# A decoder layer on one core: DMA transposes replaced by TensorE transposes and by VectorE transposes of 32-row squares with plain DMAs, in a new instruction order

## The chip, the cores and the metric

The kernel runs on one core of a Trainium2 chip. The metric is the device time of one execution in microseconds; the median over several runs is compared. Five engines run side by side, each with its own queue in program order: TensorE (PE in the profile; its weight loads are listed as PEld), VectorE (DVE), ScalarE (ACT), GpSimd (POOL) and SyncE (SP), which here only issues DMAs. Semaphores tie the queues together.

## The reference

The reference is one decoder layer over x of 16 sequences x 128 tokens x 256 features:

```
x = x + attn(layernorm(x))            # 16 heads of 64; fixed point: every product truncated to 1/4096
x = x + xattn(layernorm(x), ctx)      # 16 heads of 64, keys and values from ctx (16, 128, 128)
x = x + ffn(layernorm(x))             # 256 -> 1024 -> 256, two rank-16 experts, relu, weighted sum
```

In the first attention q, k, v, the scores, the softmax and the output go through `make_fxp`, a clip to about +-8 and a truncation to multiples of 1/4096, so those values are integers up to a scale. The second attention is ordinary softmax attention on a context. Everything is float32 outside.

## The kernel before

The 16 sequences are handled in 8 blocks (`blk`) of two sequences, 256 tokens. Each block passes through the first attention ("A"), the second ("B") and the feed-forward part ("C"). The attentions are done in two halves (`hf`) of eight heads, and within a half for one sequence (`b`) at a time. So there are 8 x 2 x 2 = 32 tiles of attention probabilities in A and 32 in B, each 128 queries x (8 heads x 128 keys).

Float32 operands are split into a high and a low f16 part (names ending in `h` and `l`), and a product takes three f16 passes. Where values are exact integers a float32 product is used.

The steps that the change and the prediction touch, with their lines in the kernel before:

- **Layer norm and input transpose**, `prep` (from L419). The normalized tile `xh` has tokens on the partitions; the following products need features there. For three of the 24 calls (`BY_PE`: A of blocks 0 and 1, C of block 7) TensorE transposes four 128x128 float32 squares into PSUM (`pt`, L449), and ScalarE and VectorE read the two f16 parts out of PSUM (L451, L452). For the other 21, ScalarE and VectorE make the two parts first (`xhi` L455, `xlo` L456) and two transposing DMAs move them (L457, L458).
- **Products q, k, v of A**, `attn_A` (from L543). Weights are scaled by 256. ScalarE reads each PSUM result twice (`trunc`, L507 and L508: the positive and the negative part, truncated into int16), and VectorE subtracts (L525 for q and k; L553 for v, to float32).
- **Probabilities of A.** After the exponential (L562) and the row sum (L564), GpSimd multiplies each head with its reciprocal and truncates to int16 (`a_A`, L571). One transposing DMA moves the tile (L574), GpSimd casts it to float32 (`aTf_A`, L576), and TensorE multiplies with v (`av_A`, L583).
- **Scores and probabilities of B**, `attn_B`. TensorE makes the scores (L540), VectorE the row extremes (`mx_B`, L641), ScalarE the exponentials and their sums (L645). GpSimd normalizes (L660) and rounds to f16 (`ah_B`, L661), VectorE subtracts for the low part (`al_B`, L662). Two transposing DMAs (L669) bring `aTh_B` and `aTl_B` for the product `av_B` (L679).
- **Output and feed-forward**: `out_proj` (`pj_A`, `pj_B`, L607), `ffn` (`u_C` L761, `dn_C` L799, the output `xo` L806 and its DMA).

The code does not run in the order in which it is written. Each step is recorded as an operation on an engine, `place` checks the dependencies along a written list of some 2,000 operation numbers (`ORDER`) and hands out buffers along it, and `emit` issues the operations in that order. The costs in the calls (`a_op`, `v_op`, `g_op`, `p_op`, `d_op`) do not enter the program. There are four sizes of SBUF buffers, `SLOTS = {"L": (4096, 9), "M": (2048, 25), "S": (1024, 26), "T": (64, 16)}` (bytes per partition and number), and two of PSUM, `PSLOTS = {"big": (4096, 3), "sml": (2048, 2)}`. A tile takes the next free buffer of its size at its first operation in the order, so an operation also waits for the last reader of the tile that had the buffer before.

Of the kernel before, what the change touches and what calls it, by code (L numbers as in the profile page):

```python
# [8 lines left out]
F32 = mybir.dt.float32  # L9
F16 = mybir.dt.float16  # L10
# [24 lines left out]
BY_PE = (("A", 0), ("A", 1), ("C", 7))  # L35
NORM_B = "PP"
# [3 lines left out]
1 29 84 85 2 20 323 86 87 324 3 14 5 0 22 325 4 326 17 88 11 327 89 6 8 15 31 90 18 91 12 7 30 42 328 92 94 93 9 19  # L40
98 99 39 16 13 23 802 100 101 10 95 149 150 142 143 102 103 40 152 151 96 104 97 54 33 126 145 144 26 562 447 128
110 153 329 127 105 111 112 106 146 41 563 147 154 129 32 148 108 113 337 330 45 155 130 338 107 131 114 564 132 109
133 43 448 44 134 331 115 381 1042 116 565 382 803 340 339 117 566 449 118 384 388 567 383 385 386 389 56 333 341
332 390 334 177 387 391 392 342 135 156 208 568 178 569 335 119 161 393 1043 804 179 157 120 621 163 162 180 394 336
164 622 628 181 182 159 158 46 623 121 624 136 183 416 160 184 165 55 185 57 137 47 1282 417 629 625 166 626 418 395
396 186 24 122 627 25 343 635 138 209 631 636 167 419 123 398 397 630 51 187 638 168 400 188 577 169 59 637 139 632
805 420 344 633 345 402 401 189 140 578 584 421 27 210 585 170 1044 347 580 579 403 171 124 634 58 190 365 346 349
586 587 172 570 366 191 173 367 28 571 192 35 36 399 581 219 351 174 422 350 404 368 175 220 141 125 640 176 423 424
34 352 405 406 369 639 370 641 193 353 407 425 642 194 643 48 354 573 221 355 454 196 371 222 455 356 195 197 198
656 37 408 456 1283 426 427 199 409 657 658 253 806 200 38 201 410 457 202 52 203 807 659 572 687 205 53 254 204 372  # L50
206 215 216 255 660 574 411 373 257 256 258 217 661 428 374 218 662 249 348 259 250 644 211 429 212 645 1045 688 251
357 252 663 808 49 60 375 261 646 260 809 927 213 376 1046 262 412 647 377 358 868 413 214 582 430 664 378 263 869
359 274 275 861 50 862 575 871 870 264 223 872 360 648 414 265 379 224 276 266 588 863 817 864 277 361 865 362 225
818 363 380 875 415 364 873 819 665 583 431 876 1048 236 278 576 666 878 237 279 877 267 226 866 432 649 820 867 238
268 874 589 879 605 227 433 896 21 591 590 667 606 821 810 239 434 607 668 1522 898 811 228 269 270 592 229 1762 897
650 669 435 593 230 651 812 813 1047 822 492 880 232 231 608 271 436 1763 240 899 824 882 609 652 881 493 241 594
825 242 1284 1049 437 438 272 653 243 207 494 439 1064 440 61 595 670 826 1065 814 596 233 827 1057 495 458 459 441
1058 597 244 273 900 245 610 1066 815 1067 883 1050 598 442 611 1051 1523 816 460 823 280 443 1068 246 234 612 1060
1059 461 884 235 901 1052 1053 671 829 445 845 599 247 600 885 613 847 444 846 654 828 488 282 831 489 902 830 490
601 496 497 281 450 614 886 498 451 1054 615 248 283 1285 903 491 500 602 1055 63 1286 1061 499 616 452 501 284 655  # L60
1108 904 453 1109 1101 617 618 1287 285 1102 502 513 1110 1111 1524 1056 603 619 832 620 887 64 604 446 905 503 888
833 462 906 848 1104 889 672 286 62 673 504 1112 1525 1103 514 1113 1289 1526 1115 1062 65 463 834 515 1063 849 1116
1288 835 505 464 1105 506 674 507 287 1118 1106 1069 836 1117 516 1107 1527 1167 1071 465 675 850 851 475 837 890
509 1529 476 288 1297 517 1070 477 1085 838 928 508 1114 1086 891 478 289 676 1087 290 466 1072 892 907 518 1120 66
908 1298 1119 893 1348 519 1121 839 1349 1300 909 467 1088 1122 840 1299 1528 510 521 1089 1351 1350 1136 852 68 468
929 469 1123 1341 677 1342 479 520 678 1290 1291 1647 511 1137 81 1138 480 471 841 1355 1764 1356 470 1352 1090 1073
894 842 481 1293 853 843 512 1091 1292 522 1344 1343 1139 472 1092 482 523 82 1301 1544 1357 1302 1358 69 1545 483
484 524 473 1546 854 83 679 70 1530 1303 1124 1547 1294 1295 680 1531 1093 1296 525 1304 1074 474 1533 1305 1353
1309 1532 855 1075 71 1345 1325 689 856 1306 844 1307 485 1327 1094 1326 486 1346 1537 1140 1311 910 72 857 1076
1538 1347 1125 487 78 1141 1354 972 1142 1328 291 1077 911 973 526 1534 292 1143 1535 1310 974 1078 895 1407 527 976  # L70
1540 858 1308 1539 1144 977 293 1329 859 975 860 1588 79 1589 1079 528 1145 1126 73 978 1095 1330 681 1360 979 1127
1541 1312 1096 1331 1536 1591 682 74 294 1590 1097 912 1542 1313 67 694 1543 686 1361 695 683 1098 75 1128 1362 1765
696 295 1080 1332 1565 1314 80 1549 685 697 684 913 76 1566 698 1081 1359 699 1146 1550 1567 690 1551 915 1315 1129
1363 691 77 1568 1581 1592 700 1593 1364 1316 692 701 914 1582 693 1130 1376 1317 1082 1318 1569 702 1147 1570 1365
1584 703 1583 1377 1148 1131 1149 1333 529 1319 1378 1132 530 1133 728 704 1595 1379 1366 1596 1585 916 1134 705
1150 531 1594 1598 1552 729 1597 1135 1151 1099 1766 1571 532 730 1083 1320 715 1100 732 1380 1084 733 1548 1367
1767 731 1553 1368 1152 1334 1768 533 736 716 1586 706 1321 1572 535 734 1587 737 738 735 1573 739 1769 917 1381
1153 1554 1322 1555 1600 717 1616 297 534 1770 1335 1154 1556 1771 296 1382 1601 1602 740 1618 1155 1617 1336 938
918 939 1773 1772 1574 298 741 1369 940 1156 1383 1603 1157 707 1337 718 1557 1777 1778 919 941 934 1558 299 1370
1338 719 536 742 1780 935 1575 1599 1779 1371 936 753 300 1158 1339 920 1576 754 301 921 1577 922 302 720 937 743  # L80
923 1559 1372 1373 1168 924 309 1384 310 708 1619 925 1578 303 755 721 1374 304 1560 1561 1774 1385 537 722 968 1775
305 1386 969 1340 1562 311 312 540 756 306 724 1387 538 1323 1324 1620 723 710 970 1781 744 709 971 541 1388 1389
711 539 930 1604 1782 1390 1776 1783 931 313 542 314 543 712 725 932 544 757 1391 1789 726 745 1805 933 1605 545
1791 1784 1806 1606 1807 1790 1375 1607 727 758 1785 980 993 759 1621 1787 1786 994 1159 1808 713 746 1392 981 1160
995 548 996 747 1393 714 307 982 1608 549 942 1161 550 1162 955 315 1622 1609 1394 308 997 1623 316 1395 318 1164
1169 956 551 1610 1163 546 317 547 1396 1165 1397 1624 943 957 319 552 1887 748 958 944 760 1212 1208 749 1213 553
1209 1214 1611 983 321 762 554 750 1579 1216 1210 751 1217 1612 959 1625 1215 1809 960 1211 1792 752 1821 1822 1626
1828 761 1218 1823 1810 984 945 1580 1613 555 1793 1829 998 1398 763 1219 1824 961 764 1825 765 1627 1628 1830 946
1408 1629 1220 1399 1400 1826 1233 1221 985 1234 1831 986 766 1630 1827 1832 1174 767 962 1401 963 947 1833 1175
1614 1222 768 1170 1648 1171 1563 988 556 1235 1834 987 964 1788 1176 1172 948 1177 1173 1402 769 1840 1856 1223 965  # L90
1409 1835 1842 1841 1811 1836 1403 1236 966 1404 989 1857 1166 949 1858 1837 1414 1838 1224 1405 926 1415 1631 558
1182 770 1794 1225 1615 1843 771 1859 1237 951 990 1410 1564 1812 967 1411 950 991 999 1416 1860 992 557 1226 1412
952 1183 1417 1413 1238 1000 1184 560 1195 1406 1185 1196 1239 1844 953 1227 1422 1001 1197 1423 1178 1179 1632 1198
1424 1845 1240 1199 1633 1813 1186 1180 1002 1846 1418 1187 1229 1795 1861 954 1634 1200 772 1181 1649 1419 1242
1435 1003 1635 1796 1241 1448 1228 1436 1243 1004 1005 1420 322 1814 1230 1636 1637 1201 1244 1425 1797 1421 1815
1231 1232 1449 1437 1456 1457 1202 1006 1188 1203 1245 1847 1798 1816 1007 1452 1458 1204 1190 1848 1799 1438 1453
1862 1638 1459 1450 1189 1451 1191 1008 1658 1639 1817 1454 1863 1659 1818 1640 1800 1192 1692 1839 1849 1660 1801
# [19 lines left out]
1037 2003 1521 1992 1986 1760 1761 2008 2010 1040 2004 1041 2012 2007 2005 2006 2009 2011 2013 2014 2015 2017 2016  # L117
2018
"""
WPOOL = ()  # L120
SPLIT_C = (7,)
WARM = 16

# [22 lines left out]
class Recorder:  # L146
    def __init__(self):
        self.ops = []
# [738 lines left out]
```

## Time and profile before

| | |
|---|---|
| median of 3 runs | 542.34 us (540.81 to 542.90) |
| the profiled execution's own time | 543.11 us |
| its span on the core | 541.3 us |
| granted TensorE clock | 1.00 |
| DMA transposes | 138 (32 `aT_A`, 64 `aTh_B` and `aTl_B`, 42 of layer-norm outputs) |

The span is the time from the first to the last instruction of the program. In the page, an engine's busy time does not count waits, branches and the issue of DMAs. In a line of a group of instructions the entries are: line of the code, engine, operation, output <- inputs (shapes), count | busy time in us, mean duration of one in ns | idle time of the engine just before them, and what ended it. In the busy time by stretches, the engines follow in the order PE, PEld, DVE, ACT, POOL, each with its number of instructions, then the granted clock, the DMA engines' share and GB/s. In a list of waits the three numbers are the total in us, the times, and the longest. In the timeline the first number is the start in us and the second the length.

### The profile page before, as it was taken

How to read it: one execution, taken by the hardware profiler on the slowest of the kernel's cores; microseconds unless marked ns; L12 is line 12 of the kernel's file. 1: busy time of each engine (PE TensorE's matmuls, PEld its weight loads, DVE VectorE, ACT ScalarE, POOL GpSimd, SP SyncE). 2: the span in 40 equal slices, each digit the busy share in tenths (PEclk: the TensorE clock that was granted, in tenths of full speed). 3: DMA queues.
4: the chain of work that ended last, by engine and by line, in shares of the span. 5: the costliest groups of instructions: out<-in, count | busy, mean ns of one | idle time of the engine just before them, and what ended most of it. 6: DMA issues, size and time to landing. Idle time of an engine off the chain costs nothing. (4 is left out here: it accounts for less than half of the span.)

```text
span 541.3 us, 15415 instructions
## 1 busy us (share of the span) xinstructions
PE 514.0 (95%) x6144; PEld 417.8 (77%) x6144; DVE 491.7 (91%) x818; ACT 457.9 (85%) x1014; POOL 337.5 (62%) x413
## 2 busy tenths in 40 slices
PE   7989997998989999999999999999999999999997
PEld 6777575877678876877777788877878788887886
DVE  5999899999999999999999988999989998986663
ACT  5999999999999999998998997879676998846331
POOL 1057436965667778646586797578967276847440
PEclk9999999999999999999999999999999999999999
DMA  8812504334452474423336126346935722691011
GB/s 283 295 41 58 142 16 107 70 60 81 75 73 51 98 148 78 99 69 41 62 76 99 23 43 106 61 79 103 150 59 105 127 51 53 116 155 22 11 40 59
DMA packets 137453, 47.17 MB, mean 87 GB/s; under 512 B 125988, under 2 KB 134438, under 8 KB 137382
## 3 DMA queue, kind: packets, MB, share of 16 engines
q1 hardware_dynamic: 137382, 46.20, 42.2%
q8 instruction: 48, 0.79, 0.6%
q14 instruction: 23, 0.19, 0.1%
HBM read 13.41 MB, written 2.10 MB: 29 GB/s over the span
## 5 line engine op out<-in xcount | busy, mean ns | idle before, releaser
L571 POOL TENSOR_SCALAR a_A<-E_A,rc_A 128x128 int16<-128x128 f32 x256 | 123.3, 503 | 49.6 <-DVE rc_A L566 27.5
L645 ACT ACTIVATE E_B<-s_B,mx_B 128x128 f32<-128x128 f32 x256 | 91.1, 419 | 6.7 <-DVE mx_B L641 3.8
L660 POOL TENSOR_TENSOR E_B<-E_B,rc_B 128x1024 f32<-128x1024 f32 x32 | 65.9, 2063 | 36.2 <-DVE rc_B L648 31.8
L645 ACT ACTIVATION_READ_ACCUMULATOR E_B<-s_B,mx_B 128x1 f32 x256 | 64.8, 259 | 0.0
L576 POOL TENSOR_SCALAR aTf_A<-aT_A 128x1024 f32<-128x1024 int16 x32 | 37.9, 1185 | 31.3 <-DMA aT_A<-a_A 18.1
L489 PEld LDWEIGHTS <-wh_A 128*128 128x128 f16 x512 | 49.2, 98 | 10.4 <-issue 2.7
L661 POOL TENSOR_SCALAR ah_B<-E_B 128x1024 f16<-128x1024 f32 x32 | 43.0, 1349 | 11.4 <-DVE al_B L662 5.7
L662 DVE TENSOR_TENSOR al_B<-E_B,ah_B 128x1024 f16<-128x1024 f32 x32 | 43.5, 1365 | 0.9 <-POOL ah_B L661 0.9
L641 DVE TENSOR_REDUCE mx_B<-s_B 128x8 f32<-128x1024 f32 x32 | 38.6, 1210 | 3.7 <-PE s_B L540 3.7
L564 DVE TENSOR_REDUCE sm_A<-E_A 128x8 f32<-128x1024 f32 x32 | 38.4, 1205 | 2.2 <-ACT E_A L562 2.2
L583 PE MATMUL av_A<-aTf_A,v_A 128*64 128x128 f32 x512 | 34.5, 278 | 4.2 <-POOL aTf_A L576 2.8
L508 ACT ACTIVATE n_sA<-s_A 128x1024 int16<-128x1024 f32 x32 | 36.6, 1183 | 2.1 <-PE s_A L540 2.1
L562 ACT ACTIVATE E_A<-p_sA 128x1024 f32<-128x1024 int16 x32 | 37.0, 1178 | 0.4 <-DVE r L779 0.4
L507 ACT ACTIVATE p_sA<-s_A 128x1024 int16<-128x1024 f32 x32 | 37.2, 1181 | 0.0
L761 PE MATMUL u_C<-xTl_C,wh_Ci 128*128 128x256 f16 x128 | 34.9, 273 | 1.2 <-DMA xTl_C<-xlo_C 1.2
L489 PE MATMUL gk_A<-xTh_A,wh_A 128*128 128x256 f16 x128 | 35.0, 273 | 1.0 <-ACT p_gA L507 0.8
L489 PE MATMUL gq_B<-xTh_B,wh_Bq 128*128 128x256 f16 x128 | 34.9, 273 | 0.9 <-DVE kl_B L625 0.8
L489 PE MATMUL gq_B<-xTl_B,wh_Bq 128*128 128x256 f16 x128 | 34.9, 272 | 0.7 <-DMA xTl_B<-xlo_B 0.7
L489 PE MATMUL gq_A<-xTl_A,wh_A 128*128 128x256 f16 x128 | 34.9, 272 | 0.5 <-DVE xTl_A L452 0.5
L761 PE MATMUL u_C<-xTh_C,wh_Ci 128*128 128x256 f16 x128 | 34.9, 273 | 0.3 <-DVE kl_B L625 0.3
L489 PE MATMUL gq_A<-xTh_A,wh_A 128*128 128x256 f16 x128 | 34.9, 273 | 0.2 <-DVE kl_B L625 0.2
L607 PE MATMUL pj_B<-wh_Bo,oh_B 128*128 128x256 f16 x128 | 34.9, 273 | 0.0
(213 smaller groups left out, 2004.4 us busy)
## 6 DMA issues: line engine op xcount, KB each, us to landing
st_A<-in_wqkvT_dram SPq DMA_DIRECT2D x6, 512.0 KB, 7.4
X<-in_x_dram SPq DMA_DIRECT2D x8, 256.0 KB, 6.3
out_dram<-xo SPq DMA_DIRECT2D x16, 128.0 KB, 1.7
st_Ap<-in_wprojT_dram SPq DMA_DIRECT2D x2, 512.0 KB, 9.3
cst<-in_ctxT_dram SPq DMA_DIRECT2D x8, 128.0 KB, 2.8
st_Bq<-in_Wq_dram SPq DMA_DIRECT2D x2, 512.0 KB, 4.3
st_Bo<-in_Wo_dram SPq DMA_DIRECT2D x2, 512.0 KB, 3.9
st_Ci<-in_wiT_dram SPq DMA_DIRECT2D x2, 512.0 KB, 3.8
```

Source lines behind the costliest of these rows:

```text
L489: PE.matmul(o[:, c, :], wv(w, i)[:, k + k0, c * 128:(c + 1) * 128], cols(acts[j], k), start=(n == 0), stop=(n == 3 * nk - 1))
L507: a_op(ncol, lambda: S.activation(p(), view(ps()), AF.Relu, bias=-LAM, scale=scale), [ps], [p], name="p")
L562: a_op(1024, lambda p=p, e=e: S.activation(flat(e()), p(), AF.Exp, bias=0.0, scale=1.0 / 4096.0), [p], [e], name="exp")
L564: v_op(1024, lambda e=e, sm=sm: V.tensor_reduce(sm(), e(), axis=AX.X, op=ALU.add), [e], [sm], name="sum")
L571: G.tensor_scalar(a()[:, h * N:(h + 1) * N], e()[:, h, :], r()[:, h:h + 1], -LAM, ALU.mult, ALU.add)
L576: g_op(1.02, lambda aT=aT, af=af: G.tensor_scalar(af(), aT(), 2.0 ** -12, 0.0, ALU.mult, ALU.add), [aT], [af], name="cast")
L641: v_op(1024, lambda ps=ps, mx=mx: V.tensor_reduce(mx(), ps(), axis=AX.X, op=ALU.min), [ps], [mx], name="max")
L645: S.activation(e()[:, h, :], ps()[:, h, :], AF.Exp, bias=mx()[:, h:h + 1], scale=-1.0, accum_out=sm()[:, h:h + 1])
L660: g_op(1.87, lambda e=e, r=r: G.tensor_tensor(e(), e(), r().unsqueeze(2).to_broadcast([128, HH, N]), ALU.mult), [r], [e], name="norm")
L661: g_op(1.02, lambda e=e, ah=ah: G.tensor_scalar(ah(), flat(e()), 1.0, 0.0, ALU.mult, ALU.add), [e], [ah], name="ahi")
L662: v_op(1024, lambda e=e, ah=ah, al=al: V.tensor_tensor(al(), flat(e()), ah(), ALU.subtract), [e, ah], [al], lock=True, name="alo")
L761: PE.matmul(ps()[:, c, :], wv(w, i)[:, k, c * 128:(c + 1) * 128], cols(xt[j], k), start=(n == 0), stop=(n == 6))
```

## The change

No DMA transposes remain; there are three replacements.

- `prep` has only the TensorE path: all 24 calls transpose on TensorE through a small PSUM buffer.
- In A, the probabilities are made with an offset of 1024, so that the int16 bits, read as f16, are transposed unchanged by TensorE against an f16 identity (`ident16`), eight heads into one small PSUM buffer (`tp_A`); ScalarE casts that to float32 (`CAST_A = "AA"`). GpSimd's cast is gone.
- In B, VectorE transposes each normalized tile in squares of 32x32 (`t1_B`), 16 plain DMAs of 32 partitions x 256 float32 carry the squares to their places (`t2_B`), and only then the tile is split into the f16 parts, on GpSimd and VectorE (`TR_B = "VV"`, `ALO = "V"`).

Besides, the weights of A are scaled by 4096 in place of 256, and v of A takes one pass on ScalarE, one on VectorE (`trunc1`) and a clamp on GpSimd instead of two on ScalarE and a subtraction on VectorE. `ORDER` is a new list. The numbers given as costs were changed in many calls. Other new branches (`S32_A`, `S32_B`, `HH_A`, `int_32`, `score_32`, `f32`, the "P" branch of `TR_B`) are switched off by their settings.

```diff
-BY_PE = (("A", 0), ("A", 1), ("C", 7))
-NORM_B = "PP"
 ORDER = """
 ...
+S32_A = ()
+S32_B = ()
+HH_A = ()
+TR_B = "VV"
+ALO = "V" 
+CAST_A = "AA"
 ...
+    ident16 = const.tile([128, 128], F16, name="ident16")
+    S.copy(ident16, ident)
 ...
-            load_weight(f"A{t}{hf}", kc(wqkvT[:, c0:c0 + 512]), 512)
+            load_weight(f"A{t}{hf}", kc(wqkvT[:, c0:c0 + 512]), 512, ws=4096.0)
 ...
-        if (key, blk) in BY_PE:
-            ps = tl("pt_" + key, "sml", [128, BLK, 2, N], F32)
-            ...
-        else:
-            xi, xl = tl("xhi_" + key, "S", [128, BLK * D], F16), tl("xlo_" + key, "S", [128, BLK * D], F16)
-            a_op(512, lambda: S.copy(xi(), fx()), [xh], [xi], name="xhi")
-            v_op(512, lambda: V.tensor_tensor(xl(), fx(), xi(), ALU.subtract), [xh, xi], [xl], lock=True, name="xlo")
-            d_op(230, lambda: SP.dma_start_transpose(th().rearrange("p b c n -> p (b c) n"), xi()), [xi], [th], name="T")
-            d_op(230, lambda: SP.dma_start_transpose(tlo().rearrange("p b c n -> p (b c) n"), xl()), [xl], [tlo], name="T")
+        ps = tl("pt_" + key, "sml", [128, BLK, 2, N], F32)
+
+        def tr():
+            for b in range(BLK):
+                for c in range(2):
+                    PE.transpose(ps()[:, b, c, :], xh()[:, b, c * 128:(c + 1) * 128], ident)
+        p_op(0.44, tr, [xh], [ps], name="tr")
+        a_op(512, lambda: S.copy(th(), ps()), [ps], [th], name="th")
+        v_op(512, lambda: V.tensor_tensor(tlo(), ps(), th(), ALU.subtract), [ps, th], [tlo], name="tl")
 ...
         v = tl("v_A", "L", [128, BLK, 512], F32)
-        pv, nv = tl("p_gA", "M", [128, 1024], I16), tl("n_gA", "M", [128, 1024], I16)
-        trunc(v_ps, pv, nv, 1024, 4096.0 / WS)
-        v_op(1024, lambda: V.tensor_tensor(flat(v()), pv(), nv(), ALU.subtract), [pv, nv], [v], lock=True, name="v")
+        trunc1(v_ps, 1024, "gA", lambda p: g_op(1.12, lambda: G.tensor_scalar(flat(v()), p(), -32767.0, None, ALU.max), [p], [v], name="v"))
 ...
-                    G.tensor_scalar(a()[:, h * N:(h + 1) * N], e()[:, h, :], r()[:, h:h + 1], -LAM, ALU.mult, ALU.add)
+                    G.tensor_scalar(a()[:, h * N:(h + 1) * N], e()[:, h, :], r()[:, h:h + 1], 1024.0 - LAM, ALU.mult, ALU.add)
             g_op(8 * 0.35, norm, [e, r], [a], name="norm")
-            aT = tl("aT_A", "M", [128, HH, N], I16)
-            d_op(460, lambda a=a, aT=aT: SP.dma_start_transpose(aT(), a()), [a], [aT], name="T")
+            tp = tl("tp_A", "sml", [128, HH, N], I16)
+            def tr(a=a, tp=tp):
+                for h in range(HH):
+                    PE.transpose(tp()[:, h, :].bitcast(F16), a()[:, h * N:(h + 1) * N].bitcast(F16), ident16)
+            p_op(8 * TR16, tr, [a], [tp], name="trA")
             af = tl("aTf_A", "L", [128, HH, N], F32)
-            g_op(1.02, lambda aT=aT, af=af: G.tensor_scalar(af(), aT(), 2.0 ** -12, 0.0, ALU.mult, ALU.add), [aT], [af], name="cast")
+            if CAST_A[b] == "A":
+                a_op(1024, lambda tp=tp, af=af: S.activation(flat(af()), flat(tp()), AF.Identity, bias=-0.25, scale=2.0 ** -12), [tp], [af], name="cast")
 ...
-            ah, al = tl("ah_B", "M", [128, HH * N], F16), tl("al_B", "M", [128, HH * N], F16)
 ...
-                g_op(1.02, lambda e=e, ah=ah: G.tensor_scalar(ah(), flat(e()), 1.0, 0.0, ALU.mult, ALU.add), [e], [ah], name="ahi")
-                v_op(1024, lambda e=e, ah=ah, al=al: V.tensor_tensor(al(), flat(e()), ah(), ALU.subtract), [e, ah], [al], lock=True, name="alo")
 ...
-            for s_, a in (("h", ah), ("l", al)):
-                t = tl(f"aT{s_}_B", "M", [128, HH, N], F16)
-                d_op(460, lambda t=t, a=a: SP.dma_start_transpose(t(), a()), [a], [t], name="T")
+                t1, t2 = tl("t1_B", "L", [128, 4, HH, 32], F32), tl("t2_B", "L", [128, 4, HH, 32], F32)
+                v_op(1024, lambda e=e, t1=t1: V.transpose(t1(), e().rearrange("p h (j b) -> p j h b", b=32)), [e], [t1], name="tr32")
+                for i in range(4):
+                    def mv(i=i, t1=t1, t2=t2):
+                        for j in range(4):
+                            SP.dma_start(t2()[32 * j:32 * j + 32, i], t1()[32 * i:32 * i + 32, j])
+                    R.op("SP", 2.0, mv, [t1], [t2], lat=3.8, name="mv", bw=128 / 330.0)
+                aT = [tl(f"aT{s_}_B", "M", [128, 4, HH, 32], F16) for s_ in "hl"]
+                g_op(1.12, lambda t2=t2, aT=aT: G.tensor_scalar(aT[0]().rearrange("p i h b -> p (i h b)"), t2().rearrange("p i h b -> p (i h b)"), 1.0, 0.0, ALU.mult, ALU.add), [t2], [aT[0]], name="ahi")
+                ...
+                    v_op(1024, lambda t2=t2, aT=aT: V.tensor_tensor(f(aT[1]), f(t2), f(aT[0]), ALU.subtract), [t2, aT[0]], [aT[1]], lock=True, name="alo")
```

## The prediction

> **What bounds the kernel now.** I read the page first (busy time by engine), then the busy time by stretches, the groups of instructions, VectorE's timeline and the chain of waits.
>
> ```profile
> PE 514.0 (95%) x6144; PEld 417.8 (77%) x6144; DVE 491.7 (91%) x818; ACT 457.9 (85%) x1014; POOL 337.5 (62%) x413
> ```
>
> TensorE and VectorE are both near the span of 541.3 us. TensorE's records overlap, so its 95% overstates it; VectorE's 491.7 is real occupation. The stretches show who sets the end, and when (columns: length, then busy of PE, PEld, DVE, ACT, POOL):
>
> ```profile
> 0.00:20.00 20.00, 16.93 (x124) 15.17 (x125) 13.80 (x31) 14.40 (x18) 2.28 (x10) 1.00 0.91 313
> 20.00:457.50 437.50, 418.67 (x5179) 333.44 (x5177) 418.70 (x716) 401.57 (x911) 295.01 (x381) 1.00 0.43 80
> 457.50:541.30 83.80, 78.43 (x847) 69.20 (x844) 59.15 (x73) 41.91 (x89) 40.22 (x22) 1.00 0.34 69
> ```
>
> Up to 457.5 us VectorE works 13.80 + 418.70 = 432.5 us and idles 25.0. After that VectorE thins out (59 of 84), and TensorE works 78.4 of 83.8, idling 5.4. So I read the span as a cut: VectorE's work up to the cut, then TensorE's work behind it: 432.5 + 25.0 + 78.4 + 5.4 = 541.3. What is added to VectorE ahead of the cut, or to TensorE behind it, is paid in full unless the idle 30.4 shrinks.
>
> **What the change takes and gives, VectorE first.** For each of the 32 tiles of the second attention a 32-row transpose of 128x1024 f32 is added. No row shows one. The nearest rows read one f32 tile of 1024 columns or write one:
>
> ```profile
> L641 DVE TENSOR_REDUCE mx_B<-s_B 128x8 f32<-128x1024 f32 x32 | 38.6, 1210 | 3.7 <-PE s_B L540 3.7
> L662 DVE TENSOR_TENSOR al_B<-E_B,ah_B 128x1024 f16<-128x1024 f32 x32 | 43.5, 1365 | 0.9 <-POOL ah_B L661 0.9
> L553 DVE TENSOR_TENSOR v_A<-p_gA,n_gA 128x1024 f32<-128x1024 int16 x16 | 21.8, 1362 | 0.5 <-ACT p_gA L507 0.5
> ```
>
> Neighbouring records overlap, so what one costs in a full queue is the step from start to start:
>
> ```profile
> 450.57 1.23 DVE L641 TENSOR_REDUCE mx_B<-s_B 128x8 f32<-128x1024 f32 x1 [0.70 <-PE s_B L540]
> 451.71 1.21 DVE L625 SCALAR_TENSOR_TENSOR ql_B<-gq_B,qh_B 128x1024 f16<-128x1024 f32 x1
> 452.84 1.22 DVE L641 TENSOR_REDUCE mx_B<-s_B 128x8 f32<-128x1024 f32 x1
> ```
>
> That is 1.14 and 1.13. I take 1.14: 32 x 1.14 = +36.5. Low end: the copies of 1024 int16 (L526 qh_A, 471 ns), 32 x 0.47 = 15.0. High end: the slowest 1024-column row (L779, 1610 ns), 51.5. A gain is excluded, since the instruction replaces none on VectorE: the subtraction that forms the low half (L662) stays, one per tile, the same size.
>
> The first attention's v (L553, 1362 ns) becomes one instruction that reads PSUM, like L625 vl_B (1204): 16 x -0.16 = -2.5. Of the input transposes 21 go over from DMA to TensorE, so xlo (6.5 + 6.1 + 4.1 = 16.7 us in all) becomes a read of PSUM like L452 (686 ns): 21 x 0.69 = 14.5, so -2.2. Sum: 491.7 + 36.5 - 2.5 - 2.2 = 523.5. In the changed order two of the 32 transposes stand behind its cut, so 30 x 1.14 - 2.5 - 2.0 = +29.7 count ahead of it.
>
> **TensorE.** Removed: nothing. Added: 256 f16 transposes (eight for each of 32 tiles, with a weight load each) and 21 x 4 f32 ones. Four f32 ones take 0.44 us in the chain of waits, so 21 x 0.44 = 9.2:
>
> ```profile
> 509.62 0.44 PE pt_C L449 x4
> ```
>
> For f16 the nearest is the score product: on 64-row halves it starts eight every 0.225 us, records of 217 ns overlapping:
>
> ```profile
> 269.65 0.39 PE L540 MATMUL s_A<-kl_A,qh_A 64*128 64x128 f16 x8
> 269.87 0.39 PE L540 MATMUL s_A<-kh_A,qh_A 64*128 64x128 f16 x8
> ```
>
> Two halves run side by side, so a full 128x128 is 0.056 us: 256 x 0.056 = 14.4, high end the f32 price of 0.11, 28.2; low end half, 7.2, if they also overlapped. TensorE gains 23.6, to 537.6 busy by its records. It stays the second engine ahead of the cut; behind it two more groups of pt_C stand than now: +0.9.
>
> A wait moves, too. TensorE's transposes of a_A wait for GpSimd. Until now it was SP's transposing DMA that waited there, with only other DMAs queued behind it:
>
> ```profile
> SPq L574 <- POOL a_A L571: 43.6, 11, 10.2
> ```
>
> On TensorE whatever product comes next in its queue would be held up instead, and VectorE behind that. I cost it at nothing because the new order can put the transposes after other products, as it does now with the products av_A, which wait 4.2 us in all for the same chain (L583); bare, the bound is those 43.6 us.
>
> The Trainium skill, "TensorE: Matmul & The Clock Gate", Part 4, gives about 275 ns for a 128x128 bf16 transpose inside a kernel. By that the 256 would cost 70.4 us and TensorE alone would need over 590; the trace's 217 ns records that start 28 ns apart say that such a figure is a latency, so I do not use it.
>
> **The others.** ScalarE: 32 casts from PSUM like L507 p_sA (1181 ns) +37.8, the second pass over v gone -18.7, the 21 casts xhi (L455, 13.3 us in all) now at xTh's 562 ns (L451) -1.5: 475.5, under VectorE and so covered. GpSimd: 32 casts gone (L576) -37.9, 16 clamps of v at that row's 1185 ns +19.0: 318.6; it is covered by VectorE, and if it were not it would gain. SP: 138 transpose issues of about 1.2 us (some 168 us) go, 512 small moves come. A plain DMA's issue is 0.316 us for 16 rows and 0.380 for an output:
>
> ```profile
> L372 SPq DMA_DIRECT2D lora_sb<-in_loraBT_dram x8: 315/316/347, 21.9 to 50.3; - x8
> DMA to landing us min/median/max: 2.0/2.5/4.2
> ```
>
> 512 x 0.32 to 0.38 = 162 to 195 us on SP, no more than now in kind. But one tile needs 16 in a row: 5.1 to 6.1, and 2.5 to land, some 8 us instead of the 3.2 that a transposed tile now takes to land. The moves wait for VectorE's transpose; queued behind them on SP are the next tile's moves, the context loads and the outputs, all due later. Then GpSimd, VectorE and TensorE wait in that order. The work of other tiles hides the extra 5 us; were it bare once, at the last tile, it would cost 5.
>
> The Trainium skill, "DMA: Bandwidth & Descriptors", Rules for kernel authors, speaks against such moves: under 64 KB a transfer is mostly overhead, and these are 32 KB. No row of this size is in the trace; by the rule the price lies in the issue and landing times above and not in bytes, so it would alter the sum by the bare 5 us at most.
>
> **Relief.** VectorE's durations lie above their group medians by 42.8 us in all (al_B: mean 1365, median 1210). GpSimd's stretch too (a_A up to 1850 ns, median 376), so part may be mutual hindrance. GpSimd loses 18.9 of 337.5 busy, VectorE 37 instructions of two SBUF inputs. Bounds 0 and -42.8; I take a tenth, -4, near the share of work that goes.
>
> **The sum.** 29.7 + 0.9 - 4 = +26.6 on the profiled span: 541.3 + 26.6 = 567.9. The profiled execution took 543.11 and the median of the runs is 542.34, 0.8 below it; 542.34 + 26.6 = **569**. It assumes that the new order idles as the old one does, 30.4 us around the cut. Even with 12 less it is 557.
>
> **Rivals.**
> - *Hindrance goes.* No crossbar writes, 32 fewer casts on GpSimd: VectorE's 42.8 us of stretch vanish. Then 541.3 + 30.6 - 42.8 = 529. It decides from a relief of over 31 of the 42.8. Against: 94% of GpSimd's busy time remains. Faster: 0.06. Halfway, with relief near 31, no change (within 0.5%, about what a measurement of this kernel can tell): 0.04.
> - *TensorE becomes the bound.* f16 transposes at 0.11: +28.2 + 9.2 = 37.4, and the new PSUM tiles (32 tp_A, 21 pt) queue for the two small PSUM buffers or wait for a_A. 514.0 + 37.4 plus its present idle 27.3 = 579. For: both engines are nearly full, and SP's 43.6 us of waiting for a_A; against: scores already run at half that price. 0.20.
> - *Buffers.* t1 and t2 take two more of the nine 4 KB buffers per tile, held through the 8 us of moves; new idle of 8 to 17: 576 to 586. The profile shows no wait for a buffer now. 0.15.
> - That transposing DMAs remain is excluded: the changed order has none.
>
> **Numbers.** My forecast has 0.55 and its own range 551 to 575: transposes at 0.5 us would give 569 - 19 = 550, at 1.61 583, so the outer range 550 to 587 holds those, TensorE's case and the buffers'. Slower 0.90, same 0.04, faster 0.06.
>
> **What would show it.** After: VectorE busy about 520 to 524; a transpose row of 32 near 1.2 us; tp_A rows on TensorE starting about 56 ns apart; ScalarE near 475, GpSimd near 319; no DMA transposes, DMA share far down. Wrong if VectorE falls under 500, if its rows other than the transpose shrink by tens of us, or if TensorE, not VectorE, has the least idle time ahead of the last 70 us.

## The result, and the profile after

The changed kernel takes 645.42 us (median of 4 runs, 643.98 to 646.37) where the kernel before took 542.62 in the same session (540.81 to 543.39): 102.8 us more, a ratio of 1.190 (95% interval 1.186 to 1.194). The forecast was 569 with a range of 550 to 587. The sign was right and the size was not. The profiled execution took 643.98 us, with a span of 642.1 and a granted clock of 0.963 where it was 1.00 before.

The busy times by engine come out almost as forecast:

```profile
PE 561.3 (87%) x6484; PEld 453.4 (71%) x6484; DVE 517.7 (81%) x850; ACT 477.9 (74%) x1031; POOL 312.8 (49%) x397
```

VectorE was forecast at 523.5, ScalarE at 475.5, GpSimd at 318.6. TensorE's 561.3 hold the lower clock: 642.1 x (1 - 0.963) = 23.8 us, if TensorE was busy in all of it, and without them it is at 537.5 (forecast 537.6). So no engine works much longer than forecast. The span of each engine is filled up with idle time: VectorE idles 124.4 us of it instead of 49.6.

The busy time by stretches, cut at the same places as before:

```profile
0.00:20.00 20.00, 16.86 (x118) 13.43 (x119) 12.30 (x26) 14.39 (x18) 3.87 (x11) 1.00 0.91 315
20.00:457.50 437.50, 387.56 (x4602) 308.20 (x4601) 378.00 (x650) 364.34 (x748) 235.51 (x328) 0.96 0.15 42
457.50:642.10 184.60, 156.84 (x1771) 131.75 (x1769) 127.43 (x176) 99.14 (x267) 73.44 (x58) 0.96 0.17 47
```

Up to 457.5 us every engine does less than before in the same time (VectorE 378.0 in place of 418.7, TensorE 387.6 in place of 418.7), though over the whole span all but GpSimd have more to do. Something holds all of them. The chain that ended last names it (shares of the span by engine, then by line):

```profile
SPq 29%; PE 28%; DVE 15%; ACT 8%; issue 7%; POOL 7%; DMA 5%; POOLq 0%; DVEq 0%; ACTq 0%
SPq L708 28%; PE pj_B L638 4%; DMA t_B<-t_B 4%; PE gk_A L493 4%; PE dn_C L849 3%; DVE aTl_B L716 3%; POOL a_A L594 3%; PE gq_B L493 2%; PE gq_A L493 2%; DVE t_B L704 2%; PE u_C L808 2%; DMA st_A<-in_wqkvT_dram 1%; ACT E_A L585 1%; PE s_A L564 1%; DVE mx_B L679 1%
```

Before, SP's queue had a share of 0%, though that chain could be followed back only to 485 us. Line L708 is the loop that issues the 16 moves of a tile. Asked for by itself, the line shows the duration of one issue (ns, min/median/max), and its landing:

```profile
L708 SPq DMA_DIRECT2D t_B<-t_B x512: 507/589/1835, 100.9 to 590.2; - x171
DMA to landing us min/median/max: 1.7/1.8/3.8
```

And SP's own timeline, late in the program (start, length, count):

```profile
504.80 40.48 SPq L708 DMA_DIRECT2D t_B<-t_B  x61
```

61 moves back to back in 40.48 us, 0.66 us each. Between 360 and 600 us the same line shows how long SP waited before its moves (the second row, ns):

```profile
L708 SPq DMA_DIRECT2D t_B<-t_B x337: 507/589/1762, 359.6 to 590.2; - x169
L708 SPq EVENT_SEMAPHORE  x26: 17/17/28, 360.2 to 572.6; - x26
```

No wait is longer than 28 ns: from 360 us on, each tile's transpose is already done when SP comes to its moves. 337 moves in 231 us are one tile per 11 us. The list of waits shows who stands behind it (total us, times, longest), and the groups show GpSimd's idle time ahead of the split:

```profile
POOL aTh_B L711 <- DMA t_B<-t_B: 97.7, 19, 10.1
...
ACT oh_B L732 <- PE av_B L726: 37.5, 14, 8.2
...
DVE aTl_B L716 <- POOL aTh_B L711: 23.8, 8, 5.3
...
DVE aTl_B L716 <- DMA t_B<-t_B: 16.6, 6, 6.7
...
DVE t_B L704 <- DMA t_B<-t_B: 10.9, 4, 7.2
```

The last of these is VectorE's transpose. Its input comes from no DMA, so this is read as waiting for a buffer that earlier moves have not yet emptied.

### The profile page after: what moved, and what is told of

The parts are those of the page before. It is cut to its first block, busy times and chain, and to the rows that moved or that the text cites. A ratio compares the mean times of both kernels' runs of the same rounds, so it can differ in the third digit from the quotient of the medians.

```text
span 642.1 us, 16573 instructions
## 1 busy us (share of the span) xinstructions
PE 561.3 (87%) x6484; PEld 453.4 (71%) x6484; DVE 517.7 (81%) x850; ACT 477.9 (74%) x1031; POOL 312.8 (49%) x397
## 4 chain that ended last, share of the span: by engine, by line
SPq 29%; PE 28%; DVE 15%; ACT 8%; issue 7%; POOL 7%; DMA 5%; POOLq 0%; DVEq 0%; ACTq 0%
SPq L708 28%; PE pj_B L638 4%; DMA t_B<-t_B 4%; PE gk_A L493 4%; PE dn_C L849 3%; DVE aTl_B L716 3%; POOL a_A L594 3%; PE gq_B L493 2%; PE gq_A L493 2%; DVE t_B L704 2%; PE u_C L808 2%; DMA st_A<-in_wqkvT_dram 1%; ACT E_A L585 1%; PE s_A L564 1%; DVE mx_B L679 1%
## 5 line engine op out<-in xcount | busy, mean ns | idle before, releaser
L594 POOL TENSOR_SCALAR a_A<-E_A,rc_A 128x128 int16<-128x128 f32 x256 | 106.0, 434 | 52.2 <-DVE rc_A L589 16.6
L711 POOL TENSOR_SCALAR aTh_B<-t_B 128x1024 f16<-128x1024 f32 x32 | 34.4, 1076 | 112.5 <-DMA t_B<-t_B 97.7
L687 POOL TENSOR_TENSOR E_B<-E_B,rc_B 128x1024 f32<-128x1024 f32 x32 | 62.2, 1946 | 44.8 <-DVE rc_B L686 38.0
L716 DVE TENSOR_TENSOR aTl_B<-t_B,aTh_B 128x1024 f16<-128x1024 f32 x32 | 47.3, 1482 | 40.4 <-POOL aTh_B L711 23.8
L576 POOL TENSOR_SCALAR v_A<-p_gA 128x1024 f32<-128x1024 int16 x16 | 48.0, 3003 | 31.3 <-DVE p_gA L518 16.6
L493 PEld LDWEIGHTS <-wh_A 128*128 128x128 f16 x512 | 50.3, 101 | 16.3 <-issue 6.2
L704 DVE STREAM_TRANSPOSE t_B<-E_B 128x1024 f32<-128x1024 f32 x32 | 39.5, 1234 | 14.1 <-DMA t_B<-t_B 10.9
L726 PEld LDWEIGHTS <-vh_B 128*64 128x64 f16 x512 | 24.8, 121 | 35.5 <-issue 25.4
L732 ACT ACTIVATE oh_B<-av_B 128x512 f16<-128x512 f32 x32 | 19.4, 612 | 37.8 <-PE av_B L726 37.5
L726 PE MATMUL av_B<-aTh_B,vh_B 128*64 128x128 f16 x256 | 27.5, 240 | 20.9 <-POOL aTh_B L711 12.2
L605 ACT ACTIVATE aTf_A<-tp_A 128x1024 f32<-128x1024 int16 x32 | 33.4, 1054 | 4.9 <-DMA t_B<-t_B 2.4
```

Source lines behind the costliest of these rows:

```text
L493: PE.matmul(o[:, c, :], wv(w, i)[:, k + k0, c * 128:(c + 1) * 128], cols(acts[j], k), start=(n == 0), stop=(n == 3 * nk - 1))
L576: trunc1(v_ps, 1024, "gA", lambda p: g_op(1.12, lambda: G.tensor_scalar(flat(v()), p(), -32767.0, None, ALU.max), [p], [v], name="v"))
L594: G.tensor_scalar(a()[:, h * N:(h + 1) * N], e()[:, h, :], r()[:, h:h + 1], 1024.0 - LAM, ALU.mult, ALU.add)
L687: g_op(1.87, lambda e=e, r=r: G.tensor_tensor(e(), e(), r().unsqueeze(2).to_broadcast([128, HH, N]), ALU.mult), [r], [e], name="norm")
L704: v_op(1024, lambda e=e, t1=t1: V.transpose(t1(), e().rearrange("p h (j b) -> p j h b", b=32)), [e], [t1], name="tr32")
L716: v_op(1024, lambda t2=t2, aT=aT: V.tensor_tensor(f(aT[1]), f(t2), f(aT[0]), ALU.subtract), [t2, aT[0]], [aT[1]], lock=True, name="alo")
```

## Experiments on the moves

Theory 1: SP issues the 512 moves one after the other at 0.59 us each, some 10 us a tile, and paces the second attention. Rivals: TensorE's added transposes in two small PSUM buffers (2), VectorE's transposes of squares (3), the clamps of v on GpSimd and the new order (4). Each kernel here is the changed kernel but for the edit shown.

**Four moves a tile, the same bytes.**

```
-                        for j in range(4):
-                            SP.dma_start(t2()[32 * j:32 * j + 32, i], t1()[32 * i:32 * i + 32, j])
+                        SP.dma_start(t2()[:, i], t1()[:, i])
```

> The same bytes leave in four moves of 128 rows per tile in place of sixteen of 32 rows (128 issues on SP in place of 512). Left out: the squares stay on their own rows, so the weights that reach the product are not wholly transposed; the amount of work on every other engine is unchanged. Theory 1 (SP's issuing, 0.59 us a move, 9.6 us a tile, paces the second attention): SP spends 128 x 0.5 to 0.6 = 64 to 77 us on the moves, GpSimd's 97.7 us of waiting for them falls under 30, and the time goes to 555 to 585 us. Theory 2 (TensorE's added transposes in two small buffers): 620 us or more, because nothing of TensorE's is changed. Theory 3 (VectorE's 39.5 us of transposes): 620 or more. Theory 4 (the 3.0 us clamps on GpSimd, and the new order): 610 or more.

Measured: 581.75 us (581.36 to 582.13), 1.072 of before (1.069 to 1.076). Of the 102.8 us, 63.7 are gone with the same bytes in a quarter of the issues. Theories 2 to 4, for which the number of issues should not matter, gave 610 and more.

```profile
L707 SPq DMA_DIRECT2D t_B<-t_B x128: 464/599/1865, 102.2 to 517.3; - x128
DMA to landing us min/median/max: 1.9/2.1/4.0
```

One issue costs the same for 128 KB (0.599 us) as for 32 KB (0.589), and the landing hardly more (2.1 against 1.8). GpSimd's 97.7 us of waiting for the moves have vanished from the list of waits.

**No moves.** The loop's body is `pass`, and the split reads `t1`.

> No moves at all: the split into two f16 parts reads VectorE's transposed squares directly. Left out: the weights that reach the product are transposed within squares of 32 rows only. Theory 1: SP is all but free and the time is what VectorE's and TensorE's work would have set, 550 to 575 us, at most 12 below the kernel with four moves. Were it the landing of a transfer, not the count of issues, that counts, this one would be more than 25 us below the kernel with four moves. Theories 2, 3 and 4: 610 us or more.

Measured: 580.36 us (580.25 to 580.48), ratio 1.070 (1.067 to 1.073), 1.4 under four moves. So with four moves a tile the landing costs next to nothing. Theory 1 holds for 65 of the 102.8 us, but its 550 to 575 was missed: some 38 us more than before remain without any move.

**The whole transposition with five DMAs a tile, through HBM** (the bounce kernel).

```
+                        if i == 0:
+                            t1.hbm = dr.tile([128, 4, HH * 32], F32, tag="tb", name=f"tb_{count[0]}", bufs=4)
+                            SP.dma_start(t1.hbm, t1().rearrange("p j h b -> p j (h b)"))
+                        if i == 1:
+                            for j in range(4):
+                                SP.dma_start(t2()[32 * j:32 * j + 32].rearrange("p i h b -> p i (h b)"), t1.hbm[:, j].rearrange("(i p) f -> p i f", p=32))
```

> The same transposition in full, with five DMAs in place of sixteen per tile: one writes the 512 KB tile of squares to HBM, four read it back, each into 32 rows at 128 KB. Theory 1: SP issues 5 x 0.6 = 3 us a tile, a tile's squares arrive after two landings of 2 to 3 us each (some 7 us in place of 11), and with 160 issues in place of 512 the time goes to 560 to 590 us. Were it the transport of a tile and not the issuing that paces it, the bounce moves twice the bytes and the time stays at 630 us or rises.

Measured: 583.47 us (583.15 to 583.79), ratio 1.076 (1.072 to 1.079). It moves twice the bytes, each tile lands twice (2.9 us each), and it is 62 us faster than the changed kernel. Its issues are cheaper, too (the read back at 128 KB):

```profile
L713 SPq DMA_DIRECT2D t_B<-tb x128: 302/424/1127, 105.2 to 521.9; - x128
```

**Two queues.** Eight of a tile's moves from ScalarE's queue, `(SP, S)[j % 2].dma_start(...)`.

> The kernel after in full, with eight of a tile's sixteen moves issued from ScalarE's queue and eight from SP's. If SP's serial issuing is the limit, a tile has left SP after 8 x 0.6 = 4.8 us in place of 9.6, SP's share of the chain falls from 29% to under 10%, and the time falls under 630 us; ScalarE pays some 256 x 0.5 = 130 us of issuing on top of its 478 busy, which puts it near 605 to 625. If the transport of 32-row moves is the limit and not the issuing, the time stays at 640 to 650 and each issue takes about twice as long.

Measured: 645.52 us (643.14 to 647.89), no gain. This is a miss for theory 1's number, and the lines tell why:

```profile
L708 SPq DMA_DIRECT2D t_B<-t_B x256: 507/590/1712, 101.7 to 580.1; - x128
L708 ACTq DMA_DIRECT2D t_B<-t_B x256: 513/602/1997, 105.9 to 588.3; - x128
```

An issue costs 0.59 to 0.60 us on either queue, so two queues do not slow each other's issues. But 256 x 0.60 = 154 us now stand in ScalarE's queue, on top of 478.5 busy: 632 of a span of 641. The expectation had charged ScalarE 130 us, at 0.5 an issue. One of its signs came true: SP's queue falls from 29% of the chain to 3%. The loss has moved to ScalarE, which with its queue now has 30% of it:

```profile
PE 32%; ACT 23%; DVE 16%; DMA 8%; ACTq 7%; issue 6%; POOL 5%; SPq 3%; DVEq 0%; POOLq 0%
```

**GpSimd's queue instead**, `(SP, G)[j % 2].dma_start(...)`.

> The kernel after in full, with half of each tile's moves issued from GpSimd's queue, the engine with the most room (313 busy of 642), in place of ScalarE's. If the price is some 0.6 us of serial issuing per move on the queue that issues it, and it hurt ScalarE because that engine was nearly full: GpSimd goes to 313 + 256 x 0.6 = 467 and the time to 590 to 625 us. If a second queue does not help as such: 635 to 650.

Measured: 666.72 us (664.20 to 669.24), 21 more than with SP alone and outside what either theory gave. GpSimd had room, and it now waits 14.5 us for moves in place of 97.7; still the kernel is slower. The issues (498 ns each) stand in the same queue as the split that the tile waits for next, but VectorE's wait for that split hardly changes (25.3 us for 23.8). What does change is VectorE's int16 subtraction, from 691 ns to this:

```profile
L529 DVE TENSOR_TENSOR p_gA<-p_gA,n_gA 128x1024 int16<-128x1024 int16 x32 | 31.8, 1000 | 1.5 <-ACT n_gA L512 1.4
```

In all, VectorE is busy 543.9 us there and 517.7 in the changed kernel, for the same instructions. That is 26 us more work, as much as would explain the 21, but where the time is lost was not shown, nor why VectorE's instructions take longer.

**The second attention by DMA transposes, as before**, the rest as changed: the f16 parts share a 4 KB buffer, and each goes through one transposing DMA.

```
-                v_op(1024, lambda e=e, t1=t1: V.transpose(t1(), ...), [e], [t1], name="tr32")
...
+                    d_op(460, lambda t=t, a2=a2, i=i: SP.dma_start_transpose(t(), a2()[:, i]), [a2], [t], name="T")
```

> The second attention's tiles are split into two f16 parts first and go through two DMA transposes each, as in the kernel before; the first attention by TensorE, the clamps on GpSimd, the order and the rest stay as in the kernel after. Theory 1: the 512 moves and VectorE's 39.5 us are gone, and the time goes to 525 to 560 us. Theory 2 (TensorE): TensorE keeps all its added work, 600 us or more. Theory 4 (clamps and order): 600 or more; a time of 560 to 600 would mean that they hold a part of the loss.

Measured: 596.78 us (596.35 to 597.22), ratio 1.100 (1.096 to 1.104). 49 us come back and 54 remain, more than without moves, though VectorE has 32 transposes less. Theory 1's 525 to 560 is missed, and the result lies in the 560 to 600 that were to mean that the clamps or the order hold a part. It is a hint, no more: the split now stands ahead of the transport, which the order was not written for.

## Experiments on the 38 to 41 us that are left

Theory A: TensorE sets the pace once SP is relieved. Theory B: VectorE with its squares does, as the prediction has it.

**No transposes of the first attention on TensorE** (the bounce kernel; ScalarE casts `a_A` itself):

```
-lambda tp=tp, af=af: S.activation(flat(af()), flat(tp()), AF.Identity, ...), [tp], [af]
+lambda a=a, af=af: S.activation(flat(af()), a(), AF.Identity, ...), [a], [af]
```

> The bounce kernel (five DMAs a tile, 583.5 us), with the first attention's 256 transposes on TensorE left out: ScalarE casts the untransposed weights straight from a_A, with the same instruction; nothing else changes. Theory A (once SP is relieved TensorE sets the pace: 547 busy of a span of 582): 256 x 0.056 = 14.4 us go, 565 to 571 us. Theory B (VectorE with its 39.5 us of squares sets it): 581 to 585.

Measured: 581.36 us (578.59 to 584.14), 2.1 under the bounce kernel and within the spread of its own two runs. TensorE has 12.9 us less busy time (534.2 for 547.1) and idles 13.1 us more. So it is theory B's number that came.

**No squares** (the kernel without moves; the split reads `E_B`):

> The kernel without moves (580.4 us), with VectorE's 32 transposes left out as well: the split into f16 parts reads E_B itself. Theory A (TensorE): VectorE gets 39.5 us of room that nobody asks for, 572 to 581 us. Theory B (VectorE): the 36.5 us that the prediction charged come back, 541 to 552.

Measured: 574.93 us (574.87 to 574.99), 5.4 under the kernel without moves. VectorE's busy time falls by 28.8 us (514.2 to 485.4), and 5.4 of that are paid back. This time it is theory A's number. So of the 36.5 us of the prediction's largest term most cost nothing here.

**Neither.**

> Both left out: no moves, no squares on VectorE, no transposes of the first attention on TensorE. What stays of the change is the new order, 21 input transposes on TensorE, the casts on ScalarE and the clamps on GpSimd. Theory A: 14 us under the kernel without squares, 558 to 567 us. Theory B: no further gain, 541 to 552. If the new order and the clamps cost nothing, the time must end at 542 + 9 for the input transposes = 551; what lies above that is theirs.

Measured: 571.53 us (570.66 to 572.40), ratio 1.054 (1.048 to 1.060). That is above what either theory gave, and 20 us above the 551 that were to mean that the order and the clamps cost nothing: with all transposes of the attention probabilities gone, 29 us of the loss are still there.

The chain of this kernel between 130 and 160 us showed what else is on the path: the clamps of v (L576) have 42% of that stretch, though only 2% of the whole chain. Their row, here of the changed kernel:

```profile
L576 POOL TENSOR_SCALAR v_A<-p_gA 128x1024 f32<-128x1024 int16 x16 | 48.0, 3003 | 31.3 <-DVE p_gA L518 16.6 <-DVE wl_Co L301 10.9 <-DVE aTl_B L716 3.4
```

They take 3.0 us each. The prediction had put 1.185 there, from the cast of the kernel before.

**The clamp as a multiply and add** (bounce kernel): `p(), -32767.0, None, ALU.max` becomes `p(), 1.0, 0.0, ALU.mult, ALU.add`.

> The bounce kernel (583.5 us) with v_A made by GpSimd as a multiply and add in place of the one maximum; left out: the clamp of v at -32767. In the trace the maximum takes 3.0 us from int16 to f32 where the cast of the kernel before took 1.19 with a multiply and add. Theory V (these 16 clamps stand on the path, as the chain of the kernel with neither shows between 135 and 157 us): the row falls to about 1.2 us, 29 us less on GpSimd, and the time falls by 8 to 16 us to 568 to 575. Theory O (what is left of the loss lies in the new order and TensorE's input transposes): 581 to 584.

Measured: 576.61 us (575.68 to 578.73), ratio 1.062 (1.059 to 1.066): 6.9 us less than the bounce kernel, a little under theory V's 8 to 16.

```profile
L577 POOL TENSOR_SCALAR v_A<-p_gA 128x1024 f32<-128x1024 int16 x16 | 19.2, 1202 | 35.2 <-DVE p_gA L519 16.6 <-DVE wl_Co L302 10.9 <-DVE aTl_B L721 7.6
```

**One part alone in the kernel before.** v by one pass and a clamp on GpSimd; the first attention's transposes on TensorE; the input transposes on TensorE. All keep the old order, and hold an instruction back only where its input or a buffer is not there yet.

> The kernel before with the part on v alone: one pass over PSUM on ScalarE in place of two, one on VectorE, and the clamp on GpSimd; all else, the order too, as before. Theory V: GpSimd gets 48 us, and a chain that had 1.36 us on VectorE has 3.0 on GpSimd: 548 to 557 us. Theory O: the clamps are hidden and ScalarE's 18.7 us fewer are worth little, 538 to 545.

> The kernel before with the first attention's transposes alone on TensorE and their casts on ScalarE, each held back until one of the two small PSUM buffers is free; all else, the order too, as before. If added work on TensorE is paid (514 busy of 541): 542 + 14.4 = 554 to 560, more where the held ones stall what is queued behind. If TensorE's added work is hidden: 540 to 547.

> The kernel before with all 24 input transposes on TensorE (3 were) in place of splitting first and two DMA transposes; all else, the order too, as before. If added work on TensorE is paid: 542 + 9.2 = 549 to 554. If hidden: 540 to 546.

Measured: 567.05 us (565.29 to 567.88; ratio 1.043, 1.040 to 1.046) for v, 607.78 (604.72 to 609.53; 1.118, 1.114 to 1.123) for the first attention, 628.36 (627.97 to 630.83; 1.159, 1.155 to 1.162) for the inputs. The work added was 46.5 us on GpSimd, which had 204 us of room, for v; 14.4 us on TensorE and 34.4 of casts on ScalarE, which had been GpSimd's, for the first attention; and 9.2 us on TensorE for the inputs. The losses are 24, 65 and 85, each above what either theory gave (the first attention's expectation left room for stalls). The steps of the order that had to be held back number 9, 38 and 60, and the losses rise with them. So none of the three can be read as the price of its part; that an order made without the part makes everything behind it wait is the likely reading, and was not tested by planning one anew.

**v again, with a fast instruction, or on VectorE**, in the kernel before:

> The kernel before with the part on v alone, as in the run that took 567.1 us, but with v_A made on GpSimd by a multiply and add in place of the maximum; left out: the clamp of v at -32767. Theory V (the 3.0 us of the maximum are what it pays, 16 times some 1.5 us of it): 543 to 550 us, most of the 24 come back. Theory O (v comes from an engine whose queue in the old order has other work in front, whatever the instruction takes): 560 to 567 us.

> The kernel before with the part on v alone and the clamp on VectorE, right behind the instruction that makes its input; in full. VectorE gains 16 x 1.2 = 19 us at most and 16 x 0.2 from the pass that it now reads from PSUM, ScalarE loses 18.7. Theory V (what counts is that v comes soon): 540 to 556, the upper end if VectorE's added work is paid in full. Theory O: 560 or more. Under 540 it would beat both kernels.

Measured: 553.76 us (551.93 to 555.06; ratio 1.020, 1.016 to 1.025) and 553.41 (551.40 to 559.17; 1.018, 1.014 to 1.023). Of the 24 us, 13 were the slow maximum; 11 stay, whichever engine makes v and although ScalarE is busy 13.6 us less (444.3 for 457.9). The first lies between the two theories, the second at the upper end of theory V's. That the 11 us are the order's is not shown: VectorE is busy 8.7 and 11.0 us more than before in these two kernels (500.4 and 502.7 for 491.7), which is as much.

**Work taken away in the new order, step by step.** From the kernel with neither: v fast; then no input transposes on TensorE; then the casts on GpSimd. In the last two, six of some 2,000 steps are held back until a buffer is free.

> The kernel with neither transposes nor moves of the weights (571.5 us), with v_A made by a multiply and add (1.2 us) in place of the maximum (3.0 us). Left out: those transposes and the clamp. In the bounce kernel the same edit gave 7 us: 563 to 567 us under both theories.

> The one before this in the list, with the 24 input transposes on TensorE left out too: the split into f16 parts reads the untransposed input from SBUF. TensorE then has the work of the kernel before, less its three input transposes. Theory W (the loss is the sum of the work that the change adds): 9 to 11 us less, 552 to 557. Theory O (the loss that is left lies in the order of the instructions, whatever their number): 561 to 567.

> The same, with the first attention's casts on GpSimd in place of ScalarE. No engine has more to do now than in the kernel before (ScalarE 15 to 19 us less, VectorE 5 less), there is no move and no DMA transpose to wait for, and only the order is the new one. Theory W: 530 to 545 us. Theory O: 555 or more; what lies above 542 is then the order's.

Measured: 569.46 us (568.00 to 570.93), 576.52 (576.41 to 576.62) and 596.43 (593.83 to 599.03). The first gives 2 us, less than the expected 4 to 8. Then the kernel without the input transposes on TensorE is 7 us slower; but VectorE's subtractions for the low part of the inputs now read SBUF in place of PSUM and take 23.4 us in place of 16.3, which is as much. Moving casts from ScalarE to GpSimd costs 20. Theory W (the loss is the sum of the added work) is refuted as a count of instructions: with no more of them than before on TensorE, VectorE and ScalarE, and 16 more on GpSimd, the last one is 53 us slower than before. Not as a sum of busy time: VectorE's is 512.1 us there and 491.7 before. Where the time goes is seen between 60 and 180 us, in the same view, first of the kernel before, then of the one with neither transposes nor moves, then of the last (length, PE, PEld, DVE, ACT, POOL, granted clock):

```profile
60.00:180.00 120.00, 110.87 (x1324) 85.75 (x1322) 115.70 (x209) 116.53 (x241) 75.55 (x111) 1.00 0.37 72
```

```profile
60.00:180.00 120.00, 97.54 (x1169) 75.53 (x1166) 104.51 (x194) 103.62 (x183) 71.18 (x100) 0.94 0.04 11
```

```profile
60.00:180.00 120.00, 91.87 (x977) 69.95 (x974) 97.50 (x173) 82.80 (x159) 59.27 (x84) 0.84 0.04 11
```

No engine is full in the second and third line, all five do less than before in the same time, and TensorE's clock is lower. This points to the fit between the order and the durations, and not to one engine's load; since no kernel with a new order was made, that is argued and not shown.

**What stays open**: how the 38 to 41 us divide between the order itself and the work it was written for. The single parts gave 5.4 (squares), 6.9 (clamps) and 2.1 (TensorE's transposes, within the spread); some 26 us are not assigned, the time by which the kernel with neither and a fast v (569.46) stands above the one before in the same session (543.78). An order planned anew for the bounce kernel was not tried. No kernel here beats the kernel before.

## Why the prediction was wrong, step by step

- **The step that failed: the moves on SP.** "512 x 0.32 to 0.38 = 162 to 195 us", "5.1 to 6.1, and 2.5 to land, some 8 us". Measured: 0.589 each, 512 x 0.589 = 302 us, and for one tile 16 x 0.59 + 1.8 = 11.2 us. The price came from rows that move other things (16 rows from HBM, an output of 128 KB), and these were taken as both ends of the range. A plain move between two places in SBUF was in no row of the trace, so the upper end should have been open; the only issues from SBUF to SBUF there, the transposing ones, took 1.23 us. And the diff itself gives four moves a cost of 2.0; if that is in us, it is 0.5 each and 8 a tile.
- **And its cover**: "The work of other tiles hides the extra 5 us; were it bare once, at the last tile, it would cost 5." That is an argument about one tile's delay. What decides is a rate. The trace of before shows how fast the second attention's tiles come late in the program, here by the instructions of line L662, one per tile:

```profile
345.00:485.00 140.00, 29.06 (x20) 1.00 0.55 97
```

  20 tiles in 140 us, one per 7.0 us. At 0.38 us a move SP needs 6.1 us a tile and keeps up; at 0.59 it needs 9.4 and does not, and then each tile adds to the queue. The kernel without moves has 19 tiles between 360 and 520 us, one per 8.4, still faster than the 11 us a tile at which SP went in the changed kernel:

```profile
360.00:520.00 160.00, 23.45 (x19) 1.00 0.01 4
```

  So the forecast stood 15% away from the point where the moves become the bound, and this rival was not among the ones named.
- **The page that spoke against it.** The Trainium skill, "DMA: Bandwidth & Descriptors", Rules for kernel authors, calls transfers under 64 KB mostly overhead. The prediction read it and let it alter "the sum by the bare 5 us at most". The runs agree with the page as far as they go: an issue cost 0.589 us for 32 KB and 0.599 for 128 KB, and a quarter of the issues gave 63.7 us.
- **A second step that failed: the idle time.** "It assumes that the new order idles as the old one does, 30.4 us around the cut." Without any move VectorE idles 64.3 us of the span where it idled 49.6 before, and is busy 514.2 where it was 491.7. So 22.5 of these 37 us are added work (forecast 31.8), and 14.7 are idle time that the forecast put at nothing. Why the new order idles more stays open. That kernel's 580.36 us lie inside the forecast's range, 11 above its middle, so the moves account for the miss of the range.
- **VectorE.** The transpose was forecast at 1.14 to 1.2 us and measured 1.234:

```profile
L704 DVE STREAM_TRANSPOSE t_B<-E_B 128x1024 f32<-128x1024 f32 x32 | 39.5, 1234 | 14.1 <-DMA t_B<-t_B 10.9 <-POOL E_B L687 3.0
```

  The term was right and its place in the sum wrong. "What is added to VectorE ahead of the cut, or to TensorE behind it, is paid in full unless the idle 30.4 shrinks": without the squares VectorE worked 28.8 us less, and 5.4 came back. So in the new order the others mostly do not wait for this part of its work.
- **TensorE.** Its busy time, less the lost clock, is 0.1 from the forecast, and the f16 transposes start 56 ns apart (median), as forecast from the score products. Its records are 223 ns long, so what the Trainium skill, "TensorE: Matmul & The Clock Gate", Part 4, gives for a transpose (275 ns) would have to be read as a latency here. The prediction's own sign of being wrong came true as it stands: up to 457.5 us TensorE idles 20 + 437.5 - 16.9 - 387.6 = 53.0 us and VectorE 67.2. But TensorE's busy time holds the lower clock there, some 0.04 x 437.5 = 17 us, and without them it idles 70. The waits that were to move to TensorE and were put at nothing, 43.6 us at most, measured 5.7: 4.6 for `a_A` and 1.1 for `tp_A`.
- **GpSimd.** The sum fits (312.8 for 318.6) by luck. The clamps took 48.0 in place of 19.0, and the rest less than before: the 256 `a_A` 106.0 in place of 123.3, the 32 splits 34.4 in place of 43.0. "It is covered by VectorE" holds only in part: in the bounce kernel 29 us less on GpSimd gave 6.9.
- **The rivals.** "TensorE becomes the bound" gave 579, and the kernels without SP's queue take 580 to 584. The number fits and the reason does not: taking 12.9 us off TensorE gave 2.1. "Buffers" would be the 10.9 us of VectorE's transposes waiting for the moves, a consequence of the slow moves.
- **The clock** was nowhere in the prediction: the kernel before has 1.00 throughout. Where TensorE waits long, it also runs slower behind the wait (last section); the changed kernel's clock was 0.963.

## What to carry to other kernels

When a change replaces one transfer by many small ones, multiply the issue time by the number per tile and hold that against the time between tiles in the busiest stretch, with an upper price that leaves room for what no row shows; a delay can be hidden, a rate cannot. Busy sums that come out right do not make the time right where engines follow a fixed order with little slack. In such a kernel an edit is priced together with its order, and moving work to an engine with room can make it slower (20 us in one run here).

## What the runs showed of the hardware that was not expected

- Issuing one DMA of 32 KB from SBUF to SBUF took 0.59 us on SP, 0.60 on ScalarE and 0.50 on GpSimd, and one of 128 KB on SP 0.60; the read of 128 KB from HBM took 0.42, the write of 512 KB 0.34.
- On GpSimd a maximum from int16 to f32 over 128x1024 took 3.0 us, a multiply and add of the same shape 1.2.
- After a gap of 6 us TensorE's granted clock was 0.50 for the next 3.5 us. In the changed kernel, in four stretches (length, then PE, PEld, DVE, ACT, POOL, clock):

```profile
404.00:410.50 6.50, 6.20 (x90) 5.42 (x90) 2.33 (x5) 6.00 (x10) 0.00 (x0) 1.00 0.19 48
410.50:416.50 6.00, 0.01 (x1) 0.03 (x1) 4.08 (x3) 0.11 (x1) 2.90 (x2) 0.80 0.18 49
416.50:420.00 3.50, 3.49 (x50) 2.73 (x50) 3.50 (x7) 1.62 (x3) 2.65 (x7) 0.50 0.21 56
420.00:424.00 4.00, 4.00 (x24) 2.26 (x23) 3.98 (x6) 3.94 (x20) 1.72 (x4) 0.89 0.19 49
```

  TensorE is idle in the second stretch, within which the clock already falls, and works at half clock in the third. Over the whole span the lower clock cost up to 23.8 us of TensorE's time.
